# A causal attention and mixture-of-experts kernel: the first block's layer norm ordered tile by tile, and three router steps moved further back

## The chip, the cores and the metric

The kernel runs on one core of a Trainium2 chip. The core has a matrix engine (TensorE, PE in the profile; PEld are its weight loads), a vector engine (DVE), a scalar engine (ACT), a general engine (POOL) and queues that issue transfers (SP among them). The metric is the device time of one execution in microseconds, the median of several runs.

## What is computed

All arrays are 32-bit floats. The input x has 4096 rows of 256. The reference is, shortened:

```python
x = L0_attn_x                                   # (1, 4096, 256)
z = layernorm(x)                                # per row, eps 1e-5
Q, K, V = z @ Qw, z @ Kw, z @ Vw
scores = Q @ K.T / sqrt(256) + causal_mask
x = x + softmax(scores) @ V
t = layernorm(x) @ W_in + b_in                  # 4096 x 256
probs = softmax(t @ W_gate + b_gate)            # 8 experts
topv, topi = top_k(probs, 2); topv /= topv.sum()
mid = relu(t @ W1[e] + b1[e])                   # 1024 wide, per chosen expert
moe = sum over the two experts of topv * (mid @ W2[e] + b2[e])
x = x + moe @ W_out + b_out
```

## The kernel before

**Tiles and stages.** A tile is 128 rows; a block is four tiles (512 rows), and there are eight blocks. A query group is 256 rows, so there are sixteen groups g, two per block b (`b, q = divmod(g, QPB)`). The attention runs over the groups; the experts' work follows as a list of items that gather the rows of one expert by index, and at the end the two experts' outputs of each row are added, multiplied with W_out and written.

**Start.** Five matmuls of zeros (`warm`, L115) are traced first. The loads of Kw, Qw and of the first four tiles of x come next. `stats0(0, 1)` traces, for each tile of block 0, its statistics on DVE (`ln_stats`, L242 and L243) and the factor on POOL (`ln_rstd`: an addition at L249, a power of -0.5 at L250). `ln_rows(0, 0, tiles=1)` traces the shift (L259) and the normalized row (L265) of each tile on DVE. `prepare_scores` (L438) transposes Qw and Kw and multiplies them into one matrix in two halves c; between the two halves it calls `turn_first`, which traces four more matmuls of zeros and then the eight transposes of block 0's normalized rows (`turn`, L287). Their copies to zT go to DVE and ACT. `project(0)` (L472) then multiplies zT with the product of the weights.

**Attention.** For group g, `scores(g)` makes the transposed score pieces (L516), a running maximum on DVE and copies on ACT. Its `finish` transposes the maximum (pt, L558), reduces it (m), spreads it (pmax, L568), and then subtracts and exponentiates the pieces. `attend(g)` (L593) multiplies the g+1 pieces with the values, four matmuls a piece and three for the last, and calls what stands in `between[c]` after piece c. Each 32-bit matmul appears as two records in the trace.

**Router.** For block b-1, `turn(1, b-1)` transposes its second layer norm into z1T (from block 2 on, DVE transposes do that instead), `enter` (ph, L323) multiplies z1T with W_in and the folded gate, DVE evacuates the logits lg and the rows hr, and SP writes hr to memory twice. `route` then finds the two best experts per row on DVE, counts the places with two small matmuls (pk, L384 and L389, from `both` and `past`), and POOL writes eight lists of slots by index (L404). With `behind=True` the first matmul of `enter` or of `route`'s count is held behind what was traced before it. `seen` is the running count. The router of blocks 0 and 1 is entered at once, before attend(2) and attend(4). From block 2 on it stands in `between[5]`, and the count of block 6 (`find`) in `between[11]` of attend(14).

**What sets the order.** The kernel is written in program order, but a planner chooses each engine's order when the program is built: it simulates the engines with its own costs, and issues what it takes as ready, earlier traced work first. The order on the chip is then fixed. `tc.keep_in_program_order(ins)` adds an edge: ins may not be issued ahead of the instruction that was traced just before it on the same engine. It makes neither of them wait for the other's end, and other work may come in between. `tc.issue_after` does the same for all instructions of a block. Waits for data are added by the framework.

**End.** `gather(b)` transposes the summed outputs of block b into two banks (pa, L1144), copies both to aT on ACT (L1149), and `leave(b)` multiplies them with W_out (pf, L1158), adds x (ot, L1166) and stores.

Of the kernel before, what the change touches and what calls it, by code (L numbers as in the profile page):

```python
# [13 lines left out]
ALU = mybir.AluOpType  # L14
# [3 lines left out]
P = 128  # L18
EPS = 1e-5
MASKED = -1e38  # L20
TB = 512
QB = 256
# [15 lines left out]
def preln_attention_moe_kernel(  # L38
# [18 lines left out]
    nc = tc.nc  # L57

    _, S, D = x.shape
    NE, _, FF = W1.shape  # L60
    NT = S // P
    NB = S // TB
    TPB = TB // P
# [30 lines left out]
    def ps_mm(name):  # L94
        return psum.tile([P, TB], F32, tag="mm", name=name, bufs=4)
# [4 lines left out]
    def ps_o(name):  # L100
        return psum.tile([P, TB], F32, tag="o", name=name, bufs=2)
# [8 lines left out]

    zeros = const.tile([P, P], F32, tag="zeros", name="zeros")
    nc.vector.memset(zeros, 0.0)

    def warm(n, pw):
        for _ in range(n):  # L115
            done = nc.tensor.matmul(
                pw[:, :QB],
                lhsT=zeros,
                rhs=zeros.unsqueeze(1).to_broadcast([P, QB // P, P]),
                start=True,  # L120
                stop=True,
            )
            tc.keep_in_program_order(done)

    warm(5, ps_mm("warm"))


    xb = [stream.tile([P, TPB, D], F32, tag=f"x{b}", name=f"x{b}") for b in range(NB)]
# [33 lines left out]
    for b in range(2, NB):  # L162
# [13 lines left out]
        out=mask,  # L176
        in_=mask,
# [8 lines left out]
    half = const.tile([P, NT], F32, tag="half", name="half")  # L186
# [50 lines left out]
        for k in range(2)  # L237
    ]

    def ln_stats(k, t):  # L240
        st = stats.tile([P, 6], F32, tag="bn", name=f"bn{k}_{t}")
        nc.vector.bn_stats(out=st, in_=xb[t // TPB][:, t % TPB, :])  # L242
        nc.vector.bn_aggr(out=lns[k][0][:, t, :], in_=st)  # L243

    def ln_rstd(k, b, tiles=TPB):

        s = ts(b, tiles)
        mv, rstd, _ = lns[k]
        nc.gpsimd.tensor_scalar_add(rstd[:, s, 0], mv[:, s, 1], EPS)  # L249
        nc.gpsimd.tensor_tensor(rstd[:, s, 0], rstd[:, s, 0], half[:, s], ALU.pow)  # L250

    def ln_rows(k, b, fill=None, tiles=TPB):

        mv, rstd, shift = lns[k]
        z = attn.tile([P, TPB, D], F32, tag=f"z{k}", name=f"z{k}_{b}", bufs=1)

        def shifts(n):
            s = ts(n, tiles)
            return nc.vector.scalar_tensor_tensor(  # L259
                shift[:, s, :], mv[:, s, 0:1], -1.0, rstd[:, s, :], ALU.mult, ALU.mult  # L260
            )

        def normalize(j):
            t = b * TPB + j
            return nc.vector.tensor_scalar(  # L265
                z[:, j, :], xb[b][:, j, :], rstd[:, t, :], shift[:, t, :], ALU.mult, ALU.add
            )

        todo = []
        for j in range(TPB):  # L270
            if j % tiles == 0:
                todo.append(partial(shifts, (b * TPB + j) // tiles))
            todo.append(partial(normalize, j))
        if fill is None:
            for do in todo:
                do()
        else:
            fill += todo
        return z

    def turn(k, b, z, zT, first=False):


        pts = [ps_mm(f"pz{k}_{b}_{c}") for c in range(ND)]
        some = [(c, j) for c in range(ND) for j in range(TPB)]
        for c, j in sorted(some, key=lambda cj: cj[1]) if first else some:
            done = nc.tensor.transpose(pts[c][:, ts(j, P)], z[:, j, ts(c, P)], ident)  # L287
            if first:
                tc.keep_in_program_order(done)
        for c in range(ND):  # L290
            if first and c:
                nc.scalar.copy(zT[:, c, :], pts[c])
            else:
                nc.vector.tensor_copy(zT[:, c, :], pts[c])
# [135 lines left out]
    zT = [attn.tile([P, ND, TB], F32, tag="kt", name=f"zT{b}", bufs=KT) for b in range(NB)]  # L430
# [27 lines left out]
                tc.keep_in_program_order(done)  # L458
            nc.vector.tensor_scalar_mul(qk_sb[:, c, :], pp[:, :D], QSCALE)

    def stats0(b, tiles=TPB):
        for t in range(b * TPB, (b + 1) * TPB):
            ln_stats(0, t)
            if (t + 1) % tiles == 0:
                ln_rstd(0, t // tiles, tiles)

    def project(b):
        qT[b] = attn.tile([P, ND, TB], F32, tag="qT", name=f"qT{b}", bufs=2)
# [116 lines left out]
    def attend(g, ss, between):  # L585

        home = ps_mm if g == NT // KU - 1 else ps_o
        po = [home(f"po{g}_{u}") for u in range(KU)]
        for c in range(g + 1):
            for k in range(KU):  # L590
                kt = c * KU + k
                for u in range(k if c == g else 0, KU):
                    nc.tensor.matmul(  # L593
                        po[u][:, : D + 1],
                        lhsT=ss[c][:, k, ts(u, P)],
                        rhs=vb[kt // TPB][:, kt % TPB, :],
                        start=(kt == 0),
                        stop=(kt == g * KU + u),
                    )
            for do in between.get(c, ()):  # L600
                do()
        for u in range(KU):
            t = g * KU + u
            rinv = attn.tile([P, 1], F32, tag="rinv", name=f"rinv{t}", bufs=4)
            nc.vector.reciprocal(rinv, po[u][:, D : D + 1])
            xt = xb[t // TPB][:, t % TPB, :]
            nc.vector.scalar_tensor_tensor(
                xt, po[u][:, :D], rinv, xt, ALU.mult, ALU.add
            )
            ln_stats(1, t)  # L610
# [362 lines left out]

    stats0(0, 1)
    first_rows = ln_rows(0, 0, tiles=1)

    def turn_first():
        warm(4, ps_o("warm2"))  # L980
        turn(0, 0, first_rows, zT[0], True)

    prepare_scores(turn_first)
    ready = project(0)
    with tc.issue_after(ready.ins):
        stats0(1)
# [43 lines left out]
    row, finish = scores(0)  # L1030
# [5 lines left out]
    for g in range(NT // KU):  # L1036
        b, q = divmod(g, QPB)

        between = {}
        nxt = None  # L1040
        if g + 1 < NT // KU:

            nxt, finish = scores(g + 1, fill)
            if g < CALM:
                finish()
            else:
                between[min(g - 2, 4)] = [partial(finish, True)]
        fill = []
        if q == 0 and b == NB - 1:

            early = seen
            tables["a"] = plan("a", early, NFULL, SB, 0)
            for n in range(AHEAD + 1):
                got[n] = fetch_rows(work[n])
        if q == 0 and b > 0:

            def send(behind=False):
                nonlocal lg
                lg = enter(b - 1, z1T, attn, behind)

            if b - 1 < TURNED[1]:
                turn(1, b - 1, rows1, z1T)
                send()
            else:
                between[5] = [partial(send, True)]
        if q == 0 and b == NB - 1:

            def fetch_first():
                for n in range(AHEAD):
                    got[n] += fetch_weights(work[n])  # L1070

            def find():
                nonlocal seen
                seen = route(b - 1, lg, seen, attn, True)

            between[6], between[11] = [fetch_first], [find]
            weighed = AHEAD
        elif q == 0 and b + 1 < TURNED[0]:
            turn(0, b + 1, ahead, zT[b + 1])
        attend(g, row, between)  # L1080
        row = nxt
        if q == 0 and b + 1 < NB:
            project(b + 1)
            values(b + 1)
            if b > 0:
                seen = route(b - 1, lg, seen, attn)
        if q == 0 and b + 2 < NB:
            stats0(b + 2)
            by_dve = b + 2 >= TURNED[0]
            ahead = ln_rows(0, b + 2, fill if by_dve else None)  # L1090
            if by_dve:
                fill += rows_todo(zT[b + 2], ahead)
        if q == QPB - 1:
            ln_rstd(1, b)
            z1T = attn.tile([P, ND, TB], F32, tag="z1T", name=f"z1T{b}", bufs=1)
            by_dve = TURNED[1] <= b < NB - 1
            rows1 = ln_rows(1, b, fill if by_dve else None)
            if by_dve:
                fill += rows_todo(z1T, rows1)
# [36 lines left out]
    def gather(b):  # L1136

        pts = [ps_tr(f"pa{b}_{c}") for c in range(ND)]
        if b > 0:
            add_up(b)  # L1140
        for i in range(2):
            for j in range(HT):
                for c in range(ND):
                    nc.tensor.transpose(  # L1144
                        pts[c][:, ts(i * HT + j, P)], accs[b, i][:, j, ts(c, P)], ident
                    )
        aT = [piece(f"aT{b}_{c}", TB) for c in range(ND)]
        for c in range(ND):
            nc.scalar.copy(aT[c], pts[c])  # L1149
        return aT  # L1150

    def leave(b, aT):
# [126 lines left out]
```

## Time and profile before

| what | value |
|---|---|
| median of three runs | 1087.06 us (1086.69 to 1088.53) |
| the profiled execution's own time | 1081.01 us |
| its span, first to last instruction | 1079.2 us |
| PE busy | 1069.7 us, 99% of the span |
| DVE busy | 728.9 us, 68% |
| ACT busy | 332.2 us, 31% |
| POOL busy | 238.4 us, 22% |
| attention's matmuls of scores, of values | 233.6 us, 237.8 us |

The profile is of one execution. In a row of the order of time, the first number is the start in microseconds from the start of the span, the second the time from the first start to the last end of the merged instructions, then engine, line, operation, output and inputs, shape and count; in brackets is the idle time of the engine before it and what ended it. In the list of waits the three numbers are the total, how often, and the longest. Ends of matmuls are modelled; starts are recorded. A stage table gives the busy time of each engine in chosen stretches of time.

### The profile page before, as it was taken

What the parts mean: (1) busy time and instruction counts of PE and PEld (TensorE: products, weight loads), DVE (VectorE), ACT (ScalarE), POOL (GpSimd) and SP (SyncE); (2) the same over time, 40 slices, a digit from 0 to 9 for tenths busy, and PEclk for the clock granted to TensorE, in tenths of its full rate; (3) what the DMA queues carried; (4) which work ended last, traced back from release to release, by engine and by line L of the source; (5) the groups of instructions that cost most, each with busy time, mean ns of one, the idle gap of its engine ahead of it and who ended that gap; (6) DMA issues with size and microseconds to landing.
All of it is one profiled execution on the core that took longest, in us unless ns stands there. A gap on an engine that the chain in (4) does not pass through costs nothing. (4 is left out here: it accounts for less than half of the span.)

```text
span 1079.2 us, 15699 instructions
## 1 busy us (share of the span) xinstructions
PE 1069.7 (99%) x5013; PEld 889.7 (82%) x5013; DVE 728.9 (68%) x2260; ACT 332.2 (31%) x731; POOL 238.4 (22%) x293
## 2 busy tenths in 40 slices
PE   9999999999999999999999999999999999999998
PEld 6878888888888888888888887787878777777887
DVE  5777788778676658255774743858588876767636
ACT  2222333332332323242402222232322432323254
POOL 2122312103103010201132522232222332313110
PEclk9999999999999999999999999999999999999999
DMA  9111001001001001000645474888879796979285
GB/s 329 59 42 40 3 1 42 1 11 32 1 1 42 1 1 40 3 1 0 187 144 181 155 241 148 274 276 259 290 253 330 254 337 208 332 224 327 80 294 189
DMA packets 121416, 151.96 MB, mean 141 GB/s; under 512 B 25581, under 2 KB 101298, under 8 KB 121332
## 3 DMA queue, kind: packets, MB, share of 16 engines
q1 hardware_dynamic: 112404, 132.84, 37.6%
q0 software_dynamic: 8384, 17.58, 5.1%
q8 instruction: 40, 0.66, 0.2%
q10 hardware_dynamic: 544, 0.52, 0.1%
q14 instruction: 44, 0.36, 0.1%
HBM read 124.79 MB, written 26.38 MB: 140 GB/s over the span
## 5 line engine op out<-in xcount | busy, mean ns | idle before, releaser
L593 PE MATMUL po<-v,s 128*128 128x257 f32 x1056 | 237.8, 380 | 0.0
L516 PE MATMUL ps<-qT,zT 128*128 128x256 f32 x1088 | 233.6, 374 | 0.0
L516 PEld LDWEIGHTS ps<-qT,zT 128*128 128x128 f32 x1088 | 203.4, 191 | 27.6 <-issue 1.3
L593 PEld LDWEIGHTS po<-v,s 128*128 128x128 f32 x1056 | 197.4, 190 | 26.2
L525 ACT COPY s<-ps 128x512 f32<-128x512 f32 x120 | 70.2, 585 | 170.7 <-PE ps L516 131.2
L948 PE MATMUL pe_a<-w_a,mid_a 128*128 128x256 f32 x544 | 121.6, 381 | 0.0
L881 PE MATMUL pm_a<-hT_a,w_a 128*128 128x256 f32 x544 | 120.0, 380 | 0.0
L948 PEld LDWEIGHTS pe_a<-w_a,mid_a 128*128 128x128 f32 x544 | 102.9, 190 | 18.7 <-issue 5.6
L890 ACT ACTIVATE mid_a<-pm_a,c_a 128x256 f32<-128x256 f32 x136 | 64.2, 472 | 169.3 <-PE pm_a L881 147.6
L881 PEld LDWEIGHTS pm_a<-hT_a,w_a 128*128 128x128 f32 x544 | 103.6, 190 | 13.8
L575 ACT ACTIVATE s<-s 128x512 f32<-128x512 f32 x120 | 71.7, 629 | 83.4 <-DVE s L572 83.1
L531 DVE TENSOR_TENSOR mx<-ps,mx 128x512 f32<-128x512 f32 x91 | 62.9, 691 | 50.8 <-ACT s L525 48.0
L861 DVE STREAM_TRANSPOSE hT_a<-h_a 32x128 f32<-32x128 f32 x272 | 82.2, 302 | 4.0
L404 POOL DMA_INDIRECT slots<-assign,ati x64 | 62.9, 983 | 84.2 <-DVE ati L402 65.6
L572 DVE TENSOR_TENSOR s<-s,pmax 128x512 f32<-128x512 f32 x120 | 73.1, 682 | 7.3 <-PE pmax L568 7.3
L957 POOL DMA_INDIRECT parts<-y_a,slot_a x34 | 34.2, 1006 | 168.2 <-DVE y_a L956 139.0
L853 DVE STREAM_TRANSPOSE mid_c<-raw_c 32x256 f32<-32x256 f32 x128 | 55.8, 436 | 1.9
L948 PE MATMUL pe_b<-w_b,mid_b 128*128 128x256 f32 x256 | 56.8, 380 | 0.0
L881 PE MATMUL pm_b<-hT_b,w_b 128*128 128x256 f32 x256 | 56.6, 380 | 0.0
L948 PEld LDWEIGHTS pe_b<-w_b,mid_b 128*128 128x128 f32 x256 | 48.6, 190 | 9.3 <-issue 2.6
L881 PEld LDWEIGHTS pm_b<-hT_b,w_b 128*128 128x128 f32 x256 | 48.7, 190 | 6.5
L890 ACT ACTIVATE mid_b<-pm_b,c_b 128x256 f32<-128x256 f32 x64 | 30.1, 471 | 63.0 <-PE pm_b L881 63.0
(283 smaller groups left out, 1232.9 us busy)
## 6 DMA issues: line engine op xcount, KB each, us to landing
w_a<-in_L_ffn_W_dram SPq DMA_DIRECT2D x68, 512.0 KB, 5.0
w_d<-in_L_ffn_W_dram SPq DMA_DIRECT2D x48, 512.0 KB, 5.4
w_c<-in_L_ffn_W_dram SPq DMA_DIRECT2D x32, 512.0 KB, 6.9
w_b<-in_L_ffn_W_dram SPq DMA_DIRECT2D x32, 512.0 KB, 7.4
rows<-hr SPq DMA_DIRECT2D x16, 512.0 KB, 4.1
yp<-parts SPq DMA_DIRECT2D x14, 512.0 KB, 11.2
x<-in_L_attn_x_dram SPq DMA_DIRECT2D x7, 512.0 KB, 7.0
out_dram<-ot SPq DMA_DIRECT2D x14, 256.0 KB, 5.2
```

The costliest lines, as they stand in the source:

```text
L404: put = nc.gpsimd.indirect_dma_start(out=slots, out_offset=bass.IndirectOffsetOnAxis(ap=ati[:, j : j + 1], axis=0), in_=assign[:, TOPK * ( ...
L516: nc.tensor.matmul(ps[:, u * QB + lo : (u + 1) * QB], lhsT=zT[kt // TPB][:, d, ts(kt % TPB, P)], rhs=qT[b][:, d, q * QB + lo : (q + 1) * Q ...
L525: nc.scalar.copy(flat, ps)
L531: done = nc.vector.tensor_tensor(mx, ps, old, ALU.max)
L572: nc.vector.tensor_tensor(s, s, pm[:, :QB].unsqueeze(1).to_broadcast([P, KU, QB]), ALU.subtract)
L575: nc.scalar.activation(s, s, AF.Exp)
L593: nc.tensor.matmul(po[u][:, : D + 1], lhsT=ss[c][:, k, ts(u, P)], rhs=vb[kt // TPB][:, kt % TPB, :], start=(kt == 0), stop=(kt == g * KU + u),
L853: pin(do())
L861: pin(do())
L881: nc.tensor.matmul(pm[:, :SB], lhsT=w1[c][:, ts(f, P)], rhs=hT[:, c, :], start=(c == 0), stop=(c == ND - 1),)
L890: nc.scalar.activation(mid[f // 2][:, f % 2, :], pm[:, :SB], AF.Relu, bias=c1[:, f : f + 1])
L948: nc.tensor.matmul(pe[ts(j, rest), :D], lhsT=mid[f][:, ts(u, P)][:, ts(j, rest)], rhs=w2[f // (NF // 2)][:, f % (NF // 2), :], start=(f == 0),
```

## The change

Four edits.

1. *First block.* The second set of zero matmuls goes, and the first five are written out in place. `stats0(0, 1)` and `ln_rows(0, 0, tiles=1)` are replaced by `first_rows`. It traces statistics and factor of tile 0, then for each next tile its statistics and factor followed by the shift and the normalized row of the tile before, and it adds an edge to each of these instructions, on DVE and on POOL. The transposes stay between the two halves of the weights' product, each held behind the one before.
2. *Router of blocks 0 and 1.* `enter` moves out of the straight line into `between[min(2 * b - 1, 5)]`: behind piece 1 of attend(2) for block 0 and behind piece 3 of attend(4) for block 1, its first matmul held there by an edge. From block 2 on it stays behind piece 5. The transposes of the next block's rows are now traced before `enter`.
3. *Last count.* `find`, the route of block 6, moves from behind piece 11 of attend(14) to behind piece 13.
4. *First output copy.* The second of the two aT copies of block 0 goes from ACT to DVE.

`between` becomes a list of lists, which alone changes no instruction.

```diff
-    def warm(n, pw):
-        for _ in range(n):
...
-    warm(5, ps_mm("warm"))
+    pw = ps_mm("warm")
+    for _ in range(5):
...
-    def ln_stats(k, t):
+    def ln_stats(k, t, keep=freely):
         st = stats.tile([P, 6], F32, tag="bn", name=f"bn{k}_{t}")
-        nc.vector.bn_stats(out=st, in_=xb[t // TPB][:, t % TPB, :])
-        nc.vector.bn_aggr(out=lns[k][0][:, t, :], in_=st)
+        keep(nc.vector.bn_stats(out=st, in_=xb[t // TPB][:, t % TPB, :]))
+        keep(nc.vector.bn_aggr(out=lns[k][0][:, t, :], in_=st))
...
-        nc.gpsimd.tensor_scalar_add(rstd[:, s, 0], mv[:, s, 1], EPS)
-        nc.gpsimd.tensor_tensor(rstd[:, s, 0], rstd[:, s, 0], half[:, s], ALU.pow)
+        keep(nc.gpsimd.tensor_scalar_add(rstd[:, s, 0], mv[:, s, 1], EPS))
+        keep(nc.gpsimd.tensor_tensor(rstd[:, s, 0], rstd[:, s, 0], half[:, s], ALU.pow))
...
+    def first_rows():
+
+        todo, keep = [], tc.keep_in_program_order
+        z = ln_rows(0, 0, todo, 1)
+        for j in range(TPB + 1):
+            if j < TPB:
+                ln_stats(0, j, keep)
+                ln_rstd(0, j, 1, keep)
+            if j:
+                for do in todo[2 * j - 2 : 2 * j]:
+                    keep(do())
+        return z
...
-    stats0(0, 1)
-    first_rows = ln_rows(0, 0, tiles=1)
-
-    def turn_first():
-        warm(4, ps_o("warm2"))
-        turn(0, 0, first_rows, zT[0], True)
-
-    prepare_scores(turn_first)
+    z = first_rows()
+    prepare_scores(lambda: turn(0, 0, z, zT[0], True))
...
             if b - 1 < TURNED[1]:
                 turn(1, b - 1, rows1, z1T)
-                send()
-            else:
-                between[5] = [partial(send, True)]
+            between[min(2 * b - 1, 5)].append(partial(send, True))
...
-            between[6], between[11] = [fetch_first], [find]
+            between[6].append(fetch_first)
+            between[13].append(find)
...
-            nc.scalar.copy(aT[c], pts[c])
+
+            (nc.vector.tensor_copy if b == 0 and c else nc.scalar.copy)(aT[c], pts[c])
```

## The prediction

> **What bounds the kernel now.** I read the page's busy shares first, then the list of what TensorE (PE) waited for, then the order of time at the places that list names.
>
> ```profile
> PE 1069.7 (99%) x5013; PEld 889.7 (82%) x5013; DVE 728.9 (68%) x2260; ACT 332.2 (31%) x731; POOL 238.4 (22%) x293
> ```
>
> PE is busy 1069.7 of 1079.2 us. An edit helps only by taking work off PE or by closing one of the gaps, 9.5 us in all. The waits of PE:
>
> ```profile
> PE ph L323 <- DVE z1T L294: 1.2, 1, 1.2
> PE pk L384 <- DVE both L375: 1.1, 1, 1.1
> ...
> PE pqk L451 <- ACT kwT L445: 0.7, 1, 0.7
> PE pf L1158 <- ACT aT L1149: 0.6, 1, 0.6
> ...
> PE pk L389 <- DVE past L379: 0.3, 1, 0.3
> ```
>
> The columns are total, times and longest. The router's matmul (ph), its count (pk) and the output matmul (pf) are places that the diff touches. Busy time also counts filler, as the start shows, in order of time (start, duration, engine, line):
>
> ```profile
> 6.96 0.21 POOL L249 TENSOR_SCALAR ln0rstd<-ln0mv 128x1 f32<-128x1 f32 x1 [0.32 <-DVE past L377]
> ...
> 7.28 2.18 POOL L250 TENSOR_TENSOR ln0rstd<-ln0rstd,half 128x1 f32<-128x1 f32 x4
> ...
> 9.01 1.81 DVE L265 TENSOR_SCALAR z<-x,ln0rstd,ln0shift 128x256 f32<-128x256 f32 x3
> 9.03 1.89 PE L116 MATMUL warm<-zeros 128*128 128x256 f32 x8
> ...
> 10.76 1.35 PE L287 MATMUL pz<-ident,z 128*128 128x128 f32 x8
> ...
> 11.01 0.60 DVE L265 TENSOR_SCALAR z<-x,ln0rstd,ln0shift 128x256 f32<-128x256 f32 x1
> ...
> 12.81 3.67 PE L472 MATMUL pq<-zT,qk 128*128 128x512 f32 x8
> ```
>
> All four powers stand behind the last of the four additions, though the first addition was done at 4.46. So the first rows come out at 9.01 and the last at 11.61, while PE multiplies zeros from 9.03 to 10.76. The first real step that PE never stops after is pq at 12.81. From 15 on the stage table has PE at 5.00 of 5, 9.74 of 10, 10.00 of 10: what pq gains is passed on.
>
> **First rows (start).** The edges force: statistics of tiles 0 and 1, shift and row 0, statistics 2, shift and row 1, statistics 3, rows 2 and 3; on POOL addition and power of each tile in turn. With this trace's durations (statistics 0.43, aggregation 0.18, addition 0.21, power 0.545, shift 0.16 and 0.22 from its start to the row's, row 0.41, handover 0.06 to 0.10) and the arrivals 3.49, 4.58, 5.71: power 0 ends 5.07, aggregation 1 ends 5.22, row 0 5.47 to 5.88. Statistics 2 follow, aggregation 2 to 6.50, row 1 6.75 to 7.16, statistics 3 and aggregation to 7.73, power 3 8.10 to 8.65, row 2 8.00 to 8.41, shift 3 8.71, row 3 8.93 to 9.34. PE finishes the first product at about 9.2 in any case, so transposes run from 9.05, the second product (0.86) follows them at about 10.0, and pq starts at 10.9: 1.9 us gained. The worst row in this stretch took 1.08 rather than 0.41 (the second of the three from 9.01, with POOL's small fills beside it). One such row in the chain puts row 3 at 10.0 and pq at about 11.2 (from the old distance, last transposes 11.67 to pq 12.81): 1.6. Two put it near 11.9: 0.9. I take 1.6, since POOL is busy with powers or fills throughout; ends 0.9 and 1.9. The eight zero records are no gain of their own: they lie beside the wait for rows, and the chain that replaces that wait is costed above. If rows came no earlier, PE would idle 1.7 us in their place. The scaled copy qk (DVE, 0.41) fits behind row 3, while PE transposes; put before row 3 it costs 0.4, inside these ends.
>
> On the clock: records of 256 columns start 0.43 apart until 8.4 and 0.216 apart from 9.03, while the granted clock reads 1.00 in every row. The change takes 1.7 us of filler away just after that step; the half pace would cost 0.21 per record. The Trainium skill, "TensorE: Matmul & The Clock Gate", Part 4 and the section on oscillation, speaks against the change: it says that transposes do not count as busy work to the clock monitor and that about 3.4 us without work halves the rate. This trace speaks partly against the first half: the rate rose at 8.4, after two microseconds of transposes. By that page the gap left (under 1 us) is too short and the cost is nothing.
>
> **Router of block 0 (in g=2).** Its matmul waits in the middle of attend(2):
>
> ```profile
> 52.61 1.03 PE L593 MATMUL po<-v,s 128*128 128x257 f32 x4
> ...
> 54.11 0.68 DVE L294 COPY z1T<-pz 128x512 f32<-128x512 f32 x1
> ...
> 54.84 0.71 PE L323 MATMUL ph<-win,z1T 128*128 128x264 f32 x2 [1.19 <-DVE z1T L294]
> ```
>
> Attend(2) has 11 matmuls, 22 records. The edge now puts 16 of them ahead of ph: 16 x 0.2165 = 3.5 us, so PE would arrive no sooner than 56.1, and the second z1T copy ends at 55.92. Gain 1.19. The count of that router is late next: ph ends about 2.1 us later (61.3 against 59.2), and PE reaches the end of the values 1.19 earlier (69.6). DVE is nearly full there (9.25 of 10 us in 50 to 60), and "both" came at 69.4, the last "past" at 71.3. If the planner leaves the count where it stood, the whole 1.19 comes back as a wait. If it puts score matmuls first, as with block 2, whose router already stands behind an edge (six score records at 176.65, count at 178.23), the price is that stretch's idle time, 50.00 - 49.88 = 0.12. I take 0.12, as the same planner, edge and chain; ends 0 and 1.19. The two row writes on SP (61.20) go some 3 us later; DMA is at 0.01 to 0.18 there, and the first gather of rows is near 536. Eight slot writes on POOL end at 84.0; the next POOL step, at 88.70, had waited 4.66 for DVE, which covers a delay of that size.
>
> **Router of block 1 (in g=4).** It had no wait. It moves behind 32 of 38 records; POOL's slot writes (119.81 to 129.7) have about 10 us free behind them. New wait of the count: by block 2's row 0.12. Upper end: ph ends at 109.9, lg and hr at 110.6, the count's chain of 4.0 (104.02 to 108.03) and behind all of DVE's other steps of 112.25 to 117.66 (5.4) it is ready at 120.0, against PE at 118.1: 1.9. I take 0.12, the nearest row; 0 to 1.9.
>
> **Last count.** Its edge moves from behind piece 11 to behind piece 13 of attend(14).
>
> ```profile
> 508.67 3.72 PE L593 MATMUL po<-v,s 128*128 128x257 f32 x16
> ...
> 516.04 3.64 PE L593 MATMUL po<-v,s 128*128 128x257 f32 x16
> ...
> 520.87 5.81 PE L593 MATMUL po<-v,s 128*128 128x257 f32 x26
> ...
> 531.18 14.92 PE L593 MATMUL po<-v,s 128*128 128x257 f32 x68
> 547.23 0.41 PE L384 MATMUL pk<-both,before 128*128 128x32 f32 x2 [1.13 <-DVE both L375]
> ```
>
> Before the count stand 16+16+26+68 = 126 records; attend(14) has 59 matmuls, 118 records. The count already stands past piece 14, so the edge binds nothing: 0, and the wait of 1.13 stays. Bounds -1.13 (the wait goes) and +1.13 (it doubles); its cover, the next attend's 126 records, is there either way.
>
> **First output copy.** The wait of 0.56 at 1042 is for the first copy, which stays on ACT (0.585). The second ended 1042.46 on ACT; on DVE it takes 0.68 (the z1T copies), 1041.4 to 1042.1, DVE being free after 1041.05. The eight pf records took 1.99 instead of 7 x 0.2165 + 0.38 = 1.90: at most 0.09 to gain; I take 0.05, at worst 0.
>
> **Sum.** -1.6 - 1.19 + 0.12 + 0.12 - 0.05 = -2.6 us. The profiled execution took 1081.01 (span 1079.2), so 1078.4; it lies 6.05 below the median of the runs, 1087.06, and the difference goes onto that: 1084.5.
>
> **Rivals.**
> 1. The count takes back the router's gain: -1.6 - 0.05 + 0.12 = -1.5, 1085.5. For it: DVE full in 50 to 70. Against: the 0.12 of block 2.
> 2. The start is not gained, because the planner threads POOL's fills and unpinned copies between the pinned steps and rows come within 0.5 us of the old time: -0.5 - 1.0 = -1.5, again 1085.5. For it: the edges fix an order, not adjacency. Against: the fills are 0.1 each and the powers cannot be gathered any more.
> 3. Slower, by the clock: PE stays at or returns to the half pace after 9.2. From 10.9 to its return each microsecond costs half of one. Against the 2.6 it decides at 5.2 us, that is 16.1; held as long as at first (1.06 to 8.4, 7.3 us, from 10.9 to 18.2) it gives +3.7 - 2.6 = +1.1, 1088.2. For it: filler goes. Against: under 1 us of gap.
> 4. New waits elsewhere: the planner's clock shifts from the start on, so positions far behind can change. One misplacement costs 1.1 to 1.2 (ph, pk); the waits listed after 20 us hold 4.0 together. Five more give +6.0 - 2.6 = +3.4, 1090.5; from four on it is beyond what can be told from no change. Against: from 200 to 500 and 615 to 1026 PE has no idle time at all, so few places are that tight.
>
> **How the numbers follow.** Chances: forecast 0.46, rival 1 0.18, 2 0.10, 3 0.08, 4 0.18. About 0.2% (2.2 us) is what can be told from no change. Faster by more: 0.42 of the forecast, 0.02 + 0.01 of rivals 1 and 2: 0.45. Slower by more: 0.05 of rival 3, 0.17 of rival 4: 0.22. Within: 0.33. The forecast's own range is 1082.7 (1.9 at the start, the 1.13 gone, no new wait, 0.09 at the end: -4.3) to 1085.2 (0.9 at the start, the rest as summed: -1.9). The wide one goes from there past rivals 1 to 3 to 1089.8, into the first part of rival 4, and leaves out some 0.04 below and 0.16 above.
>
> **What would show it.** Right: powers alternating with additions, row 3 ended by 10, no zeros after 9, pq near 11.2; ph of block 0 with no wait after 16 records; the last count still past piece 14 with its wait; pf still waiting 0.56. Wrong: pq after 12, records 0.43 apart past 11, a wait of pk near 70 or 118, or waits of PE at lines that had none.

## The result and the profile after

On the first occasion the changed kernel took 1089.44 us (median of 14 runs, 1087.00 to 1089.81) and the kernel before 1088.58 (14 runs); the ratio is 1.0002 with a 95% interval of 0.9993 to 1.0011. On a second occasion it took 1080.98 against 1081.20 (ratio 0.9994, 0.9985 to 1.0003). It makes no difference that can be measured. The profiled execution on that first occasion holds pauses of whole engines, and nearly all others there, those of before too, took as long, while the first profile of before (1081.01) has none; so parts are compared below mostly on three other occasions, where before took 1081.14 to 1081.20 and no trace has a pause.

The profiled execution after took 1087.83, span 1086.1. PE's busy time, from the page, answers to the 1069.7 of before: eight records of zeros are gone, and the time is there again.

```profile
PE 1069.9 (99%) x5005; PEld 886.5 (82%) x5005; DVE 729.3 (67%) x2261; ACT 331.6 (31%) x730; POOL 238.2 (22%) x293
```

The waits of PE (total, times, longest):

```profile
PE pm_a L893 <- ACT mid_a L902: 2.9, 1, 2.9
PE pk L397 <- DVE both L388: 1.9, 1, 1.9
PE pz L300 <- DVE z L265: 1.3, 2, 0.9
PE pmax L580 <- issue: 1.3, 1, 1.3
...
PE pz L300 <- DVE z1T L307: 0.8, 1, 0.8
PE pk L402 <- DVE past L392: 0.8, 1, 0.8
...
PE pf L1164 <- ACT aT L1155: 0.6, 1, 0.6
```

The router's wait (ph, 1.2) is gone. In its place stand a wait of transposes (pz) for the same copy z1T, a longer wait of the count for past, and a new one for the first rows. The last count's wait (pk for both, 1.9) was 1.1 in before. The waits at pm_a and pmax are pauses. The start, in order of time:

```profile
5.42 0.23 POOL L249 TENSOR_SCALAR ln0rstd<-ln0mv 128x1 f32<-128x1 f32 x1 [0.18 <-DVE past L390]
5.48 1.15 DVE L265 TENSOR_SCALAR z<-x,ln0rstd,ln0shift 128x256 f32<-128x256 f32 x1
...
5.58 0.10 POOL L1002 MEMSET rank<- 128x4 f32 x1
...
6.86 0.57 POOL L250 TENSOR_TENSOR ln0rstd<-ln0rstd,half 128x1 f32<-128x1 f32 x1
...
7.46 0.23 DVE L259 SCALAR_TENSOR_TENSOR ln0shift<-ln0mv,ln0rstd 128x1 f32<-128x1 f32 x1 [0.29 <-POOL ln0rstd L250]
...
7.74 0.87 DVE L265 TENSOR_SCALAR z<-x,ln0rstd,ln0shift 128x256 f32<-128x256 f32 x1
...
8.42 0.26 POOL L249 TENSOR_SCALAR ln0rstd<-ln0mv 128x1 f32<-128x1 f32 x1
...
9.37 0.16 DVE L259 SCALAR_TENSOR_TENSOR ln0shift<-ln0mv,ln0rstd 128x1 f32<-128x1 f32 x1 [0.21 <-POOL ln0rstd L250]
...
9.56 0.41 DVE L265 TENSOR_SCALAR z<-x,ln0rstd,ln0shift 128x256 f32<-128x256 f32 x1
...
10.22 0.16 DVE L259 SCALAR_TENSOR_TENSOR ln0shift<-ln0mv,ln0rstd 128x1 f32<-128x1 f32 x1 [0.24 <-POOL ln0rstd L250]
...
10.41 0.41 DVE L265 TENSOR_SCALAR z<-x,ln0rstd,ln0shift 128x256 f32<-128x256 f32 x1
...
12.02 0.67 PE L484 MATMUL pq<-zT,qk 128*128 128x512 f32 x1
```

Powers alternate with additions, as the edges ask. But POOL puts 24 small fills and some tables between the second tile's addition (5.42) and its power (6.86), and more of them between that power and the third tile's addition (8.42), whose statistics were ready at 7.18. The rows beside POOL's fills take 1.15 and 0.87 instead of 0.41. But both end before POOL's next power does, and the shifts of the last three rows each wait for POOL (0.29, 0.21, 0.24). So it is POOL's late powers that set the times of the rows here. PE in g=2:

```profile
52.62 0.60 PE L605 MATMUL po<-v,s 128*128 128x257 f32 x2
54.06 0.44 PE L300 MATMUL pz<-ident,z 128*128 128x128 f32 x2 [0.84 <-DVE z1T L307]
...
58.38 3.72 PE L336 MATMUL ph<-win,z1T 128*128 128x264 f32 x16
...
70.43 0.38 PE L397 MATMUL pk<-both,before 128*128 128x32 f32 x2
71.56 0.41 PE L402 MATMUL pk<-past,ones 128*128 128x32 f32 x2 [0.75 <-DVE past L392]
```

ph now starts without a wait; PE stands 0.84 at the transposes before it and 0.75 at the count behind it. And one of the pauses, far from any edit (all engines):

```profile
622.63 1.57 ACT L902 ACTIVATE mid_a<-pm_a,c_a 128x256 f32<-128x256 f32 x4 [14.18 <-remote]
623.15 5.31 PE L893 MATMUL pm_a<-hT_a,w_a 128*128 128x256 f32 x16 [2.89 <-ACT mid_a L902]
...
623.84 1.00 POOL L969 DMA_INDIRECT parts<-y_a,slot_a  x1 [3.00 <-DVE needd L647]
```

### The profile page after: what moved, and what is told of

Its sections match the earlier page's. It is cut to its first block, busy times and chain, and to the rows that moved or that the text cites. A ratio compares the mean times of both kernels' runs of the same rounds, so it can differ in the third digit from the quotient of the medians.

```text
span 1086.1 us, 15685 instructions
## 1 busy us (share of the span) xinstructions
PE 1069.9 (99%) x5005; PEld 886.5 (82%) x5005; DVE 729.3 (67%) x2261; ACT 331.6 (31%) x730; POOL 238.2 (22%) x293
```

## The experiments

The tool of comparison is the start of the same matmul in each trace, less its start in the first profile of before. It says where a microsecond comes or goes, to some 0.05. Starts also follow the arrival of the first tile: its statistics began at 3.49 in the first profile of before, at 3.43 to 3.75 in the others. Times of runs stand in the last two columns. In the three kernels with the transposes behind piece 1, the first eight or four records of the scores of g=4 stand ahead of the count, so their second column can't be set beside the others'; pq of block 3 can.

| kernel | pq of block 0 (12.81) | scores g=4 (71.56) | pq of block 3 (111.22) | experts' start (573.40) | median, us | before beside it |
|---|---|---|---|---|---|---|
| before | +0.20 | +0.20 | +0.19 | +0.18 | 1081.13 | 1081.19 |
| before, once more | +0.02 | +0.04 | +0.03 | +0.03 | 1081.16 | 1081.14 |
| changed | -0.63 | +0.40 | -0.03 | -0.02 | 1080.98 | 1081.20 |
| edit 1 alone | -0.72 | -0.73 | -0.75 | -0.75 | 1080.23 | 1081.19 |
| edit 2 alone | +0.04 | +1.05 | +0.62 | +0.60 | 1081.87 | 1081.19 |
| edit 1, fills held | -2.00 | -1.99 | -2.01 | -2.02 | 1079.07 | 1081.19 |
| edit 2, transposes behind piece 1 | +1.64 | -0.76 | +0.36 | +0.38 | 1079.83 | 1081.20 |
| edit 2, rows behind the count | -0.01 | -0.27 | -0.70 | -0.69 | 1080.45 | 1081.20 |
| last count in attend(15) | +0.14 | +0.15 | +0.15 | -1.01 | 1080.02 | 1081.20 |
| repairs together | -0.94 | -3.34 | -3.35 | -3.62 | 1081.20 | 1088.48 |
| start and last count | -2.09 | -2.08 | -1.92 | -2.21 | 1083.90 | 1088.48 |
| repairs, count behind piece 5 | -1.96 | -4.36 | -4.38 | -5.76 | 1075.27 | 1081.14 |

**Before, unchanged.**

> The kernel before, unchanged, profiled a second time. Theory A (the two profiles differ by chance): the first profile, 1079.2 us of span with the clock at full pace throughout, was an exception, since all other executions took 1086.7 or more. Then this span lies near 1086 and the trace holds a pause of all engines like the one of the changed kernel at 616 to 623 us, with a stretch of half pace behind it; the touched places stay: pq at 12.8, ph waiting 1.2 for z1T, the last count waiting 1.1. Theory B (the change costs 6.9 us): span near 1079 again, no pause. The ratio to itself gives what the timing alone can tell.

1081.13 us, ratio 0.9999 (0.9989 to 1.0009). Its trace has no pause and is the first profile of before again, 0.2 later throughout, as its first tile came 0.21 later. What was expected of a pause here fell.

**Edit 1 alone.** The rest of the kernel is that of before.

> The first edit alone (edges on the first block, no second zeros). Only the first 25 places of three engines' orders differ. Theory: pq starts at 12.0 rather than 12.8, as in the changed kernel, because POOL's fills stand between the second addition and the second power; every later landmark is 0.8 earlier until the first pause. Rival (the gain of 1.6 that was predicted needs the whole change): pq at 11.2. By time -0.8, which is too little to tell.

1080.23 us, ratio 0.9989 (0.9980 to 0.9998). Counted from the arrival of the first tile (3.65 here), pq starts 0.88 earlier, and all that follows keeps it: PE passes on what the start gains, but the start gains half of the 1.6.

**Edit 2 alone.**

```diff
             if b - 1 < TURNED[1]:
                 turn(1, b - 1, rows1, z1T)
-                send()
-            else:
-                between[5] = [partial(send, True)]
+            between[min(2 * b - 1, 5)] = [partial(send, True)]
```

> The second edit alone (router of blocks 0 and 1 behind pieces of attend). Theory: it takes back its own gain inside block 0's stretch. The wait of 1.2 of ph goes, but the transposes of the next block's rows, now ahead, wait 0.8 for a bank that z1T's copy frees, and the count waits 1.1 in its two halves instead of 0.3; the scores of g=4 start 0.8 to 1.1 later than before. Block 1 gains 0.4. Rival (the forecast): the scores of g=4 start 1.1 earlier. By time about +0.6 against -1.1.

1081.87 us, ratio 1.0007 (0.9998 to 1.0016). The scores of g=4 start 1.0 later, and block 1 gives 0.43 back. DVE's order around the count of block 0:

```profile
69.49 0.19 DVE L369 TENSOR_TENSOR hot<-hot,best 128x32 f32<-128x32 f32 x1
70.83 0.16 DVE L259 SCALAR_TENSOR_TENSOR ln0shift<-ln0mv,ln0rstd 128x4 f32<-128x4 f32 x1 [1.15 <-POOL ln0rstd L250]
70.91 0.18 DVE L375 TENSOR_TENSOR both<-hot,hot 128x32 f32<-128x32 f32 x1
71.03 0.41 DVE L265 TENSOR_SCALAR z<-x,ln0rstd,ln0shift 128x256 f32<-128x256 f32 x1
71.35 0.16 DVE L379 TENSOR_TENSOR past<-past,both 128x8 f32<-128x8 f32 x1
```

The shift of block 3's rows stands ahead of "both" and waits 1.15 for its power on POOL; three of the rows then stand between the steps of "past". In the kernel before, the same shift waited as long (1.18 at 71.02), but behind "both" and two of the three steps.

Between 51 us and the scores of g=4, PE starts 92 records in both kernels. Beyond a record's own pace (0.2165 for 256 columns, half of it for 128) PE loses 1.82 in before: 1.47 at the first ph records, 0.47 at the count, and small change of the other sign. With edit 2 it loses 2.85: 1.54 at the transposes and pt between 52.9 and 55.4, and 1.26 at the count. Of the 1.54, 1.0 stands at the transposes that wait for the copy z1T, the rest at the transposes and pt beside them. So the wait of the router became a loss around the transposes of almost the same size, and the count costs 0.79 more.

**Edit 1, with POOL's fills held behind the last power.** PE, DVE and ACT keep the order of edit 1.

```diff
+        def keep(ins):
+            last[ins.ins.engine] = ins.ins
+            return tc.keep_in_program_order(ins)
...
-    before = const.tile([P, P], F32, tag="before", name="before")
-    make_upper_triangular(nc, before, 1.0, diag=False)
+    with tc.issue_after(last[POOL]):
+        before = const.tile([P, P], F32, tag="before", name="before")
+        make_upper_triangular(nc, before, 1.0, diag=False)
```

(The other fills and tables of that stretch and the fills of v go under the same hold.)

> The first edit alone, with POOL's fills held behind the last power; PE, DVE and ACT have exactly the order of the first edit alone. Theory: the fills cost the missing half. The first normalized row, 1.15 beside the fills, takes 0.41, the second power ends near 6.0 instead of 7.4, and pq starts between 10.9 and 11.2, as predicted, 0.8 to 1.1 before the first edit alone. Rival (arrival of x sets the rows): pq stays near 12.0.

1079.07 us, ratio 0.9980 (0.9971 to 0.9989). Its start:

```profile
5.46 0.41 DVE L269 TENSOR_SCALAR z<-x,ln0rstd,ln0shift 128x256 f32<-128x256 f32 x1
...
6.54 0.41 DVE L269 TENSOR_SCALAR z<-x,ln0rstd,ln0shift 128x256 f32<-128x256 f32 x1
...
7.62 0.41 DVE L269 TENSOR_SCALAR z<-x,ln0rstd,ln0shift 128x256 f32<-128x256 f32 x1
...
8.70 0.92 DVE L269 TENSOR_SCALAR z<-x,ln0rstd,ln0shift 128x256 f32<-128x256 f32 x1
...
9.53 0.41 DVE L481 TENSOR_SCALAR qk<-pqk 128x256 f32<-128x256 f32 x1
...
10.81 1.53 PE L493 MATMUL pq<-zT,qk 128*128 128x512 f32 x3
```

Three rows take 0.41; the fourth, beside the fills that come now, 0.92. pq starts 2.1 earlier by arrival. Only POOL's order differs from edit 1 alone, so the 1.2 by which edit 1 falls short of this went to POOL's fills.

**The changed kernel, unchanged, on another occasion.**

> The changed kernel, unchanged, with the kernel before on one chip. Theory A (the pauses of 2 to 14 us in the first profile of the changed kernel belong to that occasion, not to the change): its edits' own effects add up, from the runs of the parts: pq of block 0 starts 0.7 to 0.8 earlier than in the first profile of before, scores of g=4 about 0.25 later, from pq of block 3 on 0.1 to 0.2 earlier (-0.73 of the first edit, +1.05 and -0.43 of the router edit), no gap of PE over 1.5 us between 75 and 630, a last count that waits 1.1, and at the end 0.2 less for the first output copy at most: 0.0 to 0.5 us below before. Rival B (the new order itself brings the pauses): the expert stage starts 2 us later than in before and the last matmul over 5 us later: 5 to 7 us above before.

Ratio 0.9994 (0.9985 to 1.0003). No pause; the last count waits 1.13 behind the same 126 records as before, the first pf still waits 0.56, and the last output matmul stands at -0.02, as the experts' start does: the copy on DVE brings nothing. Counted from its first tile (3.75), the parts add up: -0.88 + 1.02 - 0.43 = -0.29, against -0.28 measured.

**Edit 2, with the transposes of block 2's rows and the finish of g=3 behind piece 1 as well.**

```diff
-            if g < CALM:
+            if g == 2:
+                between[1] = [partial(turn, 0, 2, ahead, zT[2]), partial(finish, True)]
+            elif g < CALM:
                 finish()
```

(and `send` is appended to the same list.)

> Second edit alone, with the transposes of block 2's rows and the finish of g=3 in g=2 also behind piece 1 of the values, so that the router's first product is the only one that still wants the bank which the z1T copy frees. Theory (the router's matmul lost its gain because the transposes now ahead of the values wait for that bank, and the steps behind them follow): no wait of PE between 50 and 63 us, pq of block 1 or 2 in that place 1.0 to 1.2 earlier than in before, scores of g=4 about 1.0 earlier, from pq of block 3 on 1.0 to 1.4 earlier; about -1.2 us. Rival (the loss is in the count alone, which DVE answers late wherever the transposes stand): the wait near 54 goes, but the count near 70 waits as much longer, and scores of g=4 start within 0.3 of before or later.

1079.83 us, ratio 0.9984 (0.9975 to 0.9993). In the profiled execution the last tile of x came late (its statistics waited until 7.86), so pq of block 0 is 1.64 late; the runs are not. From pq of block 0 on, pq of block 2 comes 1.59 earlier and pq of block 3 1.28 earlier than in before.

```profile
53.37 1.06 PE L287 MATMUL pz<-ident,z 128*128 128x128 f32 x8
54.26 3.64 PE L593 MATMUL po<-v,s 128*128 128x257 f32 x16
57.74 1.04 PE L287 MATMUL pz<-ident,z 128*128 128x128 f32 x8
...
60.35 3.73 PE L323 MATMUL ph<-win,z1T 128*128 128x264 f32 x16
...
73.56 0.38 PE L384 MATMUL pk<-both,before 128*128 128x32 f32 x2 [0.87 <-DVE both L375]
```

The 16 records of values now stand ahead of the transposes as well and cover the copy; both waits near 54 are gone. The count is late all the same, 0.87, even behind eight score records. The rival had that half right.

**Edit 2, with block 3's shift and rows held behind block 0's count on DVE.**

```diff
+            if b == 1:
+                with tc.issue_after(counted[0]):
+                    ahead = ln_rows(0, b + 2)
+            else:
+                ahead = ln_rows(0, b + 2, fill if by_dve else None)
```

> Second edit alone, with the shift and the normalized rows of block 3 on DVE held behind the last step of block 0's count (the running count). The order on PE is that of the second edit alone. Theory (the two waits of the count near 70, 0.35 and 0.75, come from DVE steps of the next block's rows that were put between the count's own steps): both waits go, scores of g=4 start 1.1 earlier than with the second edit alone, which is about 0.05 earlier than before, and the wait of 0.84 for the bank near 54 stays; from pq of block 3 on 0.4 to 0.5 earlier than before if the rows still come in time, later if PE then waits for them. Rival (the late logits are what holds the count): its waits stay over 0.7, scores of g=4 still 0.7 or more later than before.

1080.45 us, ratio 0.9994 (0.9985 to 1.0003). The count stands without a wait, the transposes still wait, and the scores of g=4 start 1.3 earlier than with edit 2 alone:

```profile
54.85 0.44 PE L287 MATMUL pz<-ident,z 128*128 128x128 f32 x2 [0.84 <-DVE z1T L294]
...
70.92 0.30 PE L388 MATMUL pk<-both,before 128*128 128x32 f32 x2
71.06 0.39 PE L393 MATMUL pk<-past,ones 128*128 128x32 f32 x2
```

So the count was not held by late logits, but by the rows that were put among its steps.

**The kernel before, with the last count behind piece 2 of attend(15).**

```diff
-            between[6], between[11] = [fetch_first], [find]
+            between[6] = [fetch_first]
...
+        elif g == NT // KU - 1:
+            between[2] = [find]
```

> The kernel before with only the last count moved, to behind piece 2 of attend(15) in place of piece 11 of attend(14); between pieces 11 and 13 of attend(14), the third edit, the order is the same on every engine. Theory (the count's own DVE chain ends 1.1 after PE gets there, and 16 to 24 more records of 0.2165 ahead of it cover this): its wait goes from 1.1 to 0, and the expert stage starts 1.1 earlier; about -1.1 us. Rival (the slots, the gathers behind them or the first expert's matmuls wait in its place): the expert stage starts within 0.3 of before, with a new wait of PE at its first matmuls.

1080.02 us, ratio 0.9992 (0.9983 to 1.0001); the experts start 1.16 earlier by arrival. The count, which waited 1.13 behind 126 records, stands behind 142 without a wait, and nothing later waits for it:

```profile
531.35 18.39 PE L593 MATMUL po<-v,s 128*128 128x257 f32 x84
549.58 0.30 PE L384 MATMUL pk<-both,before 128*128 128x32 f32 x2
549.92 0.41 PE L389 MATMUL pk<-past,ones 128*128 128x32 f32 x2
```

**Repairs together, and the start with the last count.** The first holds the edits of the four kernels above that mended something (fills, transposes, rows, last count) and leaves the copy on ACT; the second has no router edit.

> All repairs together: first edit with POOL's fills held behind the last power, second edit with transposes and finish behind piece 1 and with block 3's rows held behind block 0's count, last count behind piece 2 of attend(15). If the parts do not touch each other they add up: -2.0 (start) -1.25 (transposes behind piece 1, counted from its own pq of block 0) -0.7 or more (the count's wait of 0.87 that was left there) -1.15 (last count) = -5.1 us, some 1076.1 beside a before of 1081.2, with no wait of PE over 0.3 between 10 and 560 us. If something else is late next (DVE, nearly full from 50 to 75), scores of g=4 start less than 3.5 earlier than in before, with a wait of PE in its stead: -3.2 to -4.5.

> The same without any router edit: the first edit with the fills held, and the last count behind piece 2 of attend(15). If the two add up: pq of block 0 at 10.8 to 10.9, ph still with its wait of about 1.2 near 52, the last count without a wait, expert stage 3.1 to 3.2 earlier than in before: -3.15 us, about 1078.0 beside 1081.2. The difference to the kernel with all repairs is then what the router edit is worth once repaired: 1.9 or more if the theory holds, under 1 if not.

These two ran on an occasion with pauses: before took 1088.48, they 1081.20 (ratio 0.9942, 0.9928 to 0.9955) and 1083.90 (0.9965, 0.9953 to 0.9977). Up to the experts the traces can be read. The first lost 1.1 of its start to a late last tile (statistics at 7.93); from its pq of block 0 on, pq of block 3 comes 2.41 earlier than in before, and in the second 0.17 later: the repaired router edit, that of block 1 included, is worth some 2.4. The last count still waits in both:

```profile
546.06 0.30 PE L410 MATMUL pk<-both,before 128*128 128x32 f32 x2
547.31 0.41 PE L415 MATMUL pk<-past,ones 128*128 128x32 f32 x2 [0.94 <-DVE past L403]
```

In both, its chain on DVE holds an idle 0.93 ahead of the reciprocal of attend(14) (at 541.82 in the first). The changed kernel has 0.69 at that place in its first profile and none in its second, and the kernel with the late count alone has none: this idle time came with the occasions that hold pauses, and its cause is open.

**Before again, and all repairs with the count behind piece 5 of attend(15).**

> The kernel before, unchanged. Theory (the pause near 610 to 620 of the first profile of the changed kernel is no part of the change): if this occasion holds pauses at all, this kernel's profile shows one at the same step of the program, with ACT, SP, POOL and DVE all idle for microseconds and PE waiting 2 to 3 for mid_a, and its runs lie at 1086 to 1092; if it holds none, the expert stage from 573.5 to the last matmul takes as in the first profile of before and the runs lie at 1081. Rival (the pause comes with the changed order): no such pause here, while the kernel beside it shows one.

> All repairs together once more, with the last count behind piece 5 of attend(15) in place of piece 2: 24 records more ahead of it, 5.2 us, against the 0.94 that it still waited for past there. Theory: that wait goes to 0, the expert stage starts 0.9 earlier than with all repairs, set against the scores of g=15; router part as before, scores of g=4 earlier by 2.4 beside the gain of pq of block 0. In an occasion without pauses, with the last tile of x arriving as in before: -2.0 -2.4 -1.2 = -5.6 us, some 1075.6 beside 1081.2. Rival (the gathers behind the count or the expert's first matmuls wait in its place): the expert stage starts no earlier, with a wait of PE at its first matmuls.

No pauses came on this occasion, so whether the kernel before pauses at the same step remains unseen in a trace. With all repairs it takes 1075.27 us against 1081.14: ratio 0.9943 (0.9929 to 0.9956), 5.9 us below before, which the changed kernel only equals. Start -1.96, router -2.42 up to pq of block 3, last count -1.38. All waits of PE that are left (total, times, longest):

```profile
PE warm L116 <- DVE zeros L112: 1.1, 1, 1.1
PE pqk L477 <- ACT kwT L471: 0.7, 1, 0.7
PE pz L309 <- DVE z L269: 0.6, 1, 0.6
PE pf L1185 <- ACT aT L1176: 0.6, 1, 0.6
PE pm_z L907 <- PEq L1256: 0.4, 1, 0.4
PE pqwT L470 <- DMA qw<-in_L_attn_Qw_dram: 0.4, 1, 0.4
PE ph L345 <- DVE z1T L560: 0.3, 1, 0.3
PE pnc L653 <- DVE countb L655: 0.2, 1, 0.2
```

## Why the prediction held in its range and was wrong in its sum

The likeliest case was "faster", at 1084.5; measured was no change, and 1089.44 lies inside 1082.7 to 1089.8, near its upper end. 1.5 of the 4.9 between them is the base: before's median was 1087.06 over three runs and 1088.58 over fourteen. 2.3 is the sum, -2.6 forecast and -0.3 measured. The other 1.1 is left over from the first occasion, where the changed kernel lay 0.86 above before, within the interval, and not 0.2 below it as on the second. That 1089.44 lies inside the range is luck as far as the mechanism goes: its upper part was meant for a slower clock and for waits far behind the edits, and neither came. Term by term:

- **First rows, -1.6 forecast, -0.88 measured.** The order of the chain was right: row 0 was put at 5.47 and began at 5.48. The step that failed is that POOL takes each addition and power as soon as its input is there: "power 3 8.10 to 8.65" ran from 9.61 to 10.18. The second power came 1.2 after its addition was done, and the third addition 1.2 after its statistics, both behind fills, and PE waited 1.3 for rows. The margin, "I take 1.6, since POOL is busy with powers or fills throughout", was counted in slow rows. Two rows were slow (1.15 and 0.87), but POOL was later than they were; that two slow rows had been put near 11.9 as the lower end, and pq came at 12.02, is luck. "PE finishes the first product at about 9.2 in any case" was wrong too: it ended at 8.43, and at 8.6 and 8.4 in the second and third profile of before; PE waited for rows behind it. Rival 2 named this cause, that an edge fixes an order and not adjacency, but priced it at 0.5 left of the gain where 0.88 was left, and its argument against ("the powers cannot be gathered any more") overlooked that fills can stand between an addition and its power. Holding the fills brought 2.1, beyond my upper end of 1.9.
- **Router of block 0 with its count, -1.19 + 0.12 forecast, +1.02 measured.** "PE would arrive no sooner than 56.1" was right for ph, which waits no more. The failed step is "Gain 1.19": I counted what the edge puts ahead of ph, and not what is then traced ahead of the values. The transposes of block 2's rows need the bank that the first z1T copy frees, so they met the same DVE copy at the same time (1.54 lost around them, 1.0 of it at that copy, against 1.47). Moving them behind piece 1 as well gave 1.59 at pq of block 2.
- **Of that its count alone, +0.12 forecast with 1.19 as the upper end, +0.79 measured.** Rival 1 was right that the count waits, with the wrong reason: not the later logits, but the next block's shift, which waits for POOL, and its rows, which were ordered ahead of the count's steps. Holding those removed the wait. The failed argument is "the same planner, edge and chain": the edge and the chain are those of block 2, but what DVE has to do beside them is not.
- **Router of block 1, +0.12 forecast, -0.43 measured.** The count went behind two score records and didn't wait. In before, PE lost 0.30 ahead of pmax at 108.78 and small gaps around ph in this group; they went. I had given the move no chance of a gain.
- **Last count, 0 and 0.** Between 120 and 1040 us no engine's order in the changed kernel's trace differs from before, so the third edit bound nothing, and the wait of 1.13 stayed; the 1.92 of the first profile after was not there in the second. That this wait could be had at all I had in the bounds only; it took a move by 16 records.
- **First output copy, -0.05 forecast, 0.00 measured.** The wait is for the first copy, as said.
- **Rival 3** did not come: the records of the second product start 0.21 apart (from 11.16), and the eight of pq took 3.67 in both kernels. The granted clock, 1.00 in all rows up to 620, can't tell it: it reads 1.00 from 1 to 5 in before too, where the records of zeros stand 0.43 apart. The prediction's reading that the rate rose at 8.4, after two microseconds of transposes, doesn't hold either. The first profile of before has no records of 256 columns between 5.1 and 8.07. In its second profile the transposes of the weights start 0.11 apart from 5.78 on, where the first has 0.21. So the moment differs between executions of one kernel, and no run here shows whether transposes count as work for the clock.
- **Rival 4** did not come: from pq of block 3 to the last output matmul the changed kernel keeps its distance to before within 0.01 where no pause falls.

## What to carry to other kernels

When a wait is moved out of the way, list what else wants the same producer or the same buffer and will now stand in its place: here the transposes wanted the bank that the copy was to free, and most of the wait went over to them. An edge that keeps an order lets other work in between; if the pinned chain is what counts, the early-ready fills on its engines, and the next stage's steps on a shared engine, have to be held behind it. Where PE is 99% busy, look for what waits are left, even of 1 us or less, with enough independent records within reach: the start, the routers of blocks 0 and 1 with their counts, and the last count gave 5.9 us together once repaired, while the four edits as made gave 0.3.

## What the runs showed of the hardware

- **Rows beside fills.** A normalized row (DVE, from and to on-chip memory) takes 0.41 alone or beside a power, whether the power starts behind it (row at 9.56, power at 9.61 in the changed kernel) or is already running (power from 8.88 to 9.46, row at 9.01 in before). Beside POOL's fills and tables of 0.1 to 0.3 it took 0.48 to 1.15. The scaled copy qk, which reads a matmul bank, takes 0.41 beside POOL's tables (9.53 above) and beside its fills of v (11.54 in before). The Trainium skill, "SBUF — State Buffer", section "SBUF: two separate sides", says that VectorE and GpSimd lock one pair of ports for a whole instruction, and that only some VectorE instructions need the pair. The rows beside fills and the copy agree with that; the row that began while a power was running and kept its 0.41 does not. That the lock is what slows the rows is not shown.
- **Pauses.** On two of five occasions traces hold stretches in which engines stand together at fixed steps of the program. Near 610 to 623, ACT was idle 14.2, POOL 3.0 and PE 2.9 in each of three traces (the first of the changed kernel, and the two kernels of the later occasion), and in none of the eleven others, the first profile of before among them. They cost 4.7 (changed kernel), 3.2 and 4.8 us there. The runs of before on the same occasions took 1086.7 to 1092.0, and those of the later one have a mean granted clock of 0.995 to 0.998, where all but three of 103 on other occasions have 0.999 or 1.000. This suggests that before pauses too; no trace shows it. The four later occasions each used another chip, so chip and occasion can't be told apart, and the cause is open.
- **The clock after such a gap.** PE stood 2.89, 2.92 and 2.89. Behind the first and the third, the granted clock reads 0.50 in the stretches 624 to 626 and 620 to 622, and the next 16 records took 5.31 and 5.37; behind the second it stays at 1.00, and they took 3.72. That is the 1.6 by which its pause cost less. The Trainium skill, "TensorE: Matmul & The Clock Gate", section "HAM oscillation — how this bites in real kernels", warns of idle gaps above about 3.4 us; here 2.9 was enough in two of three cases.
- **Arrival.** In two of fourteen traces the last tile of block 0 came near 7.9, and DVE waited 1.04 and 1.35 for it, where it otherwise had it without waiting. This cost pq 1.1 and 1.6.
